# Third layer's experts: tiles ordered by the tokens they hold, and six of eight blocks of results added, turned and stored between the last tiles

## The chip, the core and the metric

The kernel runs on one core of one Trainium2 chip. The metric is the device time of one execution in microseconds (us), as the median of several runs. The kernel before took 3433.5 us (median of three runs, 3429.64 to 3435.67).

The engines: PE is TensorE (PEld is its weight load), DVE is VectorE, ACT is ScalarE, POOL is GpSimd, and SP is the engine that here only issues DMAs. "SPq" and "ACTq" are the instruction queues of SP and ACT, where they issue DMAs.

## The reference, cut to what matters

The whole network is an image of 256 channels and 64 x 64 places (4096 tokens) that passes through two convolution layers, an attention layer with experts, and a second attention layer with experts. Only the last stage is touched: for each token, two of eight experts are chosen, each expert is a two-layer product with a GELU between, and the two weighted results are added to the token. Then tokens become channels again.

```python
gate_logits = xf @ Wg + bg
top_w, top_i = jax.lax.top_k(gate_logits, TOP_K)          # TOP_K = 2 of E = 8 experts
top_w = jax.nn.softmax(top_w, axis=-1)
...
for e in range(E):
    h = jax.nn.gelu(xf @ W1[e] + b1[e], approximate=False)    # 256 -> 1024
    out = out + w_dense[:, e:e + 1] * (h @ W2[e] + b2[e])     # 1024 -> 256
```

## The kernel before

**Tokens and blocks.** The 4096 tokens live on the chip in `t` (128 partitions x 32 rows of 256). A block is 512 tokens (`NB`), so there are eight (`NBLK`), each of four rows of 128 (`TPB`). The output is written as channels, one block of 512 columns at a time.

**From tokens to experts' tiles.** `route` (L2028, L2039) finds both experts of each token and scatters its row into `xs` in DRAM, where each expert has a list. `S["cum"]` counts how many rows each expert has so far. A tile is 256 rows of one expert's list (`MT`). There are at most 39 tiles (`NTILE`); 36 are always run (`MOST`), and the last three stand under a condition (L2279) and are skipped where the counts need no more. In this profile they are skipped.

**Two lists of tiles.** The first 20 tiles (`FULL`) are full with tokens of blocks 0 to 6 alone, whatever the data, so their list ("A", `full_table`, L2125) is made while the attention of the last block still runs. The others are listed in "B" by `tile_table` (L2157) as one of the `steps` that `attn3` hands to the experts. Both lists go expert by expert. The lists hold, for each tile, the row in `xs` and the expert; for a tile that is not full, `in` and `off` send the rows beyond the end to a place that nobody reads.

**The loop over tiles** (`expert_tiles`, L2282). Iteration i loads rows four tiles ahead and weights two ahead (both on SP's queue), then does `first(i)`, 32 matmuls into `f_h_ps` with a GELU on ACT (L2320); four transposes of tile i+1's rows (L2254) whose copy is L2255 on DVE; and `second(i-1)`, 56 matmuls into `f_ya_ps` and `f_yb_ps`, the additions on DVE (L2375 to L2384), a scaling on ACT (L2391), and two scatters on POOL (L2392) into `ys` in DRAM, one row for each token and choice. `sides` (L2349) prepares combinations of weights on POOL. Two steps are taken in each iteration while any are left; PE's order is as written until the last step has been taken, and from then on a planner orders all engines by priority (place in the program) and by when it thinks inputs are there. Until then PE alone is fixed; the others are the planner's.

**The end.** After the last tile and the condition, `store` (L1365) takes the eight blocks in turn. For each it loads the block's two results out of `ys` (`outputs`, L2438, one half by SP, one by ACT, 512 KB each), adds token and results in PSUM by three transposes into each place (`to_channels`, L244, so 24 for a block), copies half 0 with ACT (L254) and half 1 with DVE (L256), and stores 512 KB (L1375). In `to_channels` a half of four places fills one bank of PSUM.

A read of `ys` waits for all scatters ahead of it in the program, since a scatter's rows are known only at run time. For the same reason a scatter behind a read waits until that read has landed.

Of the kernel before, what the change touches and what calls it, by code (L numbers as in the profile page):

```python
# [10 lines left out]
F32 = mybir.dt.float32  # L11
BF16 = mybir.dt.bfloat16
I32 = mybir.dt.int32
AF = mybir.ActivationFunctionType
ALU = mybir.AluOpType
# [4 lines left out]
P = 128  # L20
C = 256
# [71 lines left out]
class Net:  # L93
# [1270 lines left out]

    def store(self, t, out, more=False):  # L1365

        with (
            self.tc.tile_pool(name="st", bufs=3) as pool,
            self.tc.tile_pool(name="st_ps", bufs=2, space=PSUM) as ps,
        ):  # L1370
            for b in range(NBLK):
                o = pool.tile([P, 2, NB], F32, tag="o", name="st_o")
                y = self.outputs(b, pool.tile([P, 2, TPB, C], F32, tag="g", name="f_g")) if more else None
                self.to_channels(ps, "ps", t[:, b * TPB : (b + 1) * TPB, :], o, *([y[:, 0], y[:, 1]] if more else []))
                self.nc.sync.dma_start(out=out.rearrange("(m p) n -> p m n", p=P)[:, :, b * NB : (b + 1) * NB], in_=o)  # L1375

# [582 lines left out]
    def moe_consts(self, pool):  # L1963
# [6 lines left out]
                                channel_multiplier=-1, compare_op=ALU.is_ge, fill=0.0)  # L1970
        i = pool.tile([P, NTILE], I32, tag="count_i", name="count_i")
        nc.gpsimd.iota(i, pattern=[[1, NTILE]], base=0, channel_multiplier=0)
        self.count = pool.tile([P, NTILE], F32, tag="count", name="count")
        nc.vector.tensor_copy(self.count, i)
# [64 lines left out]
    def route_parts(self, t0, T, t, S, wp, n, nT, bank):  # L2039
# [47 lines left out]
        def count():  # L2087
            hot = got["hot"]
            both = got["both"] = room("f_both")[:, :T]
            nc.vector.tensor_add(both, hot[:, 0], hot[:, 1])  # L2090

            cum = got["cum"] = wp.tile([P, TPB + 1, NE], F32, tag="f_cum", name="f_cum")
            if t0 == 0:
                nc.vector.memset(cum[:, 0, :], 0.0)
            else:
                nc.vector.tensor_copy(cum[:, 0, :], S["cum"])
            for i in range(T):
                nc.vector.tensor_add(cum[:, i + 1, :], cum[:, i, :], both[:, i, :])
            S["cum"] = cum[:, T, :]

# [23 lines left out]

    def full_table(self, S, wp, bank):  # L2125

        nc = self.nc
        T, n = S["A"], FULL
        tl = lambda shape, tag, dt=F32: wp.tile([P] + shape, dt, tag="f_" + tag, name="f_" + tag, bufs=1)
        c_ps = bank()[:, :NE]  # L2130
        self.mm(c_ps, [(self.all_one, S["cum"])])
        ci = tl([NE], "ci", I32)
        nc.vector.tensor_copy(ci, c_ps)
        nc.vector.tensor_single_scalar(ci, ci, MT.bit_length() - 1, ALU.arith_shift_right)
        full = tl([NE], "cnt")
        nc.vector.tensor_copy(full, ci)
        ends = tl([NE], "ends")
        nc.vector.tensor_tensor_scan(ends, self.one.to_broadcast([P, NE]), full, 0.0, ALU.mult, ALU.add)
        past = tl([NTILE, NE], "past")[:, :n]
        nc.vector.tensor_tensor(past, bc(ends, 1, n), bc(self.count[:, :n], 2, NE), ALU.is_le)  # L2140
        nc.vector.tensor_reduce(T["ex"], past, AX.X, ALU.add)
        nc.vector.tensor_scalar_mul(T["tab"][:, 0, :], T["ex"], float(P))
        nc.vector.tensor_tensor(past, past, bc(full, 1, n), ALU.mult)
        tau = tl([NTILE], "tau")[:, :n]
        nc.vector.tensor_reduce(tau, past, AX.X, ALU.add)
        nc.vector.tensor_sub(tau, self.count[:, :n], tau)
        nc.vector.tensor_scalar_mul(tau, tau, float(MT))
        nc.vector.scalar_tensor_tensor(tau, T["ex"], float(N), tau, ALU.mult, ALU.add)
        nc.vector.tensor_copy(T["tab"][:, 1, :], tau)
        gone = S["gone"]  # L2150
        nc.vector.tensor_sub(gone, full, ends)
        nc.vector.tensor_scalar(gone, gone, float(n), 0.0, ALU.add, ALU.max)
        nc.vector.tensor_tensor(gone, gone, full, ALU.min)
        nc.gpsimd.memset(T["in"], 1.0)
        nc.gpsimd.memset(T["off"], 0.0)

    def tile_table(self, S, wp, bank, early=False):  # L2157


        nc = self.nc  # L2160
        T = S["B"]
        n = NTILE - FULL if early else NTILE
        tl = lambda shape, tag, dt=F32: wp.tile([P] + shape, dt, tag="f_" + tag, name="f_" + tag, bufs=1)
# [8 lines left out]
        nc.vector.tensor_copy(cnt, ci)  # L2172
        if early:
            nc.vector.tensor_sub(cnt, cnt, S["gone"])
        ends = tl([NE], "ends")
# [15 lines left out]
        nc.vector.tensor_sub(tau, tau, skip)  # L2191
        if early:
            nc.vector.tensor_tensor(past, bc(ex, 2, NE), bc(self.count[:, :NE], 1, n), ALU.is_equal)
            nc.vector.tensor_tensor(past, past, bc(S["gone"], 1, n), ALU.mult)
            nc.vector.tensor_reduce(skip, past, AX.X, ALU.add)
            nc.vector.tensor_add(tau, tau, skip)
        nc.vector.tensor_scalar_mul(tau, tau, float(MT))
# [14 lines left out]
        nc.vector.tensor_tensor(ins, bc(self.nth[:, :NI], 1, n), bc(skip, 2, NI), ALU.is_lt)  # L2212
        nc.vector.tensor_scalar(off, ins, -1.0, 1.0, ALU.mult, ALU.add)
        for i in range(0, n, 4):
            k = min(4, n - i)
            part = off[:, i : i + k, :].rearrange("p i k -> p (i k)")
            nc.vector.scalar_tensor_tensor(part, self.nth[:, : k * NI], float(2 * N), part, ALU.add, ALU.mult)

# [18 lines left out]
    def expert_where(self, T, j, x, tl):  # L2237
# [6 lines left out]
        op.tensor_tensor(to, x[:, :, C], second, ALU.add)  # L2244
        op.tensor_tensor(to, to, T["in"][:, j, :], ALU.mult)
        op.tensor_tensor(at, to, T["off"][:, j, :], ALU.add)
        op.tensor_tensor(first, first, x[:, :, C + 1], ALU.mult)
# [34 lines left out]
    def expert_tiles(self, S, order, wp, ps, steps, early, pre, written):  # L2282
# [119 lines left out]

        nc.scalar.activation(wp.tile([P, 1], F32, tag="g", name="f_gelu", bufs=1), self.one, AF.Gelu)
        xs, ws = {}, {}
        for i in tiles[:ahead_x]:
# [13 lines left out]
        for i in tiles:  # L2419
            if i + ahead_x <= tiles[-1]:  # L2420
                xs[i + ahead_x] = rows(i + ahead_x)
            if i + ahead <= tiles[-1]:
                ws[i + ahead] = weights(i + ahead)
            w1, w2 = ws.pop(i)
            xs.pop(i)
            h = first(xT, w1, (pre["ahead"][1:] if i == 0 else ()) if steps else None)
            now = (i, h, w2, sides(w2)) + to
            step()
            if i < tiles[-1]:
                xT = turn(xs[i + 1])  # L2430
                to = where(i + 1, xs[i + 1])
            if done is not None:
                second(*done)
                step()
            done = now
        second(*done)

    def outputs(self, b, y):  # L2438

        src = self.ys[: 2 * N, :].rearrange("(r b p i) c -> b p r (i c)", r=2, b=NBLK, i=TPB)  # L2440
        for r in range(2):
            (self.nc.sync, self.nc.scalar)[r].dma_start(out=(y[r] if isinstance(y, list) else y[:, r]).rearrange("p i c -> p (i c)"), in_=src[b][:, r])
        return y
# [9 lines left out]
    def moe_state(self, pool, L=2):  # L2453
        tl = lambda shape, tag, dt=F32: pool.tile([P] + shape, dt, tag=tag, name="f_" + tag)
        return {
            "L": L, "to": tl([2, NT], "to", I32), "used": tl([1], "used", I32),
            "big": tl([2, 2, NT // 2], "big"), "r": tl([NT], "r"), "gone": tl([NE], "gone"),
            **{k: {"tab": tl([2, n], "tab" + k, I32), "ex": tl([n], "ex" + k), "in": tl([n, NI], "in" + k), "off": tl([n, NI], "off" + k)}
               for k, n in (("A", FULL), ("B", NTILE))},
        }  # L2460
# [35 lines left out]

    def attn3(self, t, S):

# [5 lines left out]
        with (  # L2504
# [28 lines left out]
            if True:  # L2533
# [230 lines left out]
                with tc.manual_schedule(engines={ET.PE, ET.Pool}):  # L2764
                    steps = iter(())
                    for g in range(first, G + LAG):
# [6 lines left out]
                        if b > 0:  # L2773
# [6 lines left out]
                            if b == NBLK - 1 and j == TPB + 5:  # L2780
                                self.full_table(S, keep, bank)
                                one = lambda shape, tag: keep.tile([P] + shape, F32, tag=tag, name="f_" + tag, bufs=1)
# [8 lines left out]
            last = route((NBLK - 1) * TPB, TPB)  # L2791
            go = lambda: next(last, None)
            self.experts(
                S, [go] * 5 + [lambda: self.tile_table(S, keep, bank, True)],
                {**pre, "ahead": [lambda i=i: finish(NBLK - 1, i) for i in range(TPB)]},
            )

    def limits3(self, S, pool):
# [86 lines left out]
    def run(self, x, out):  # L2885
        tc, nc = self.tc, self.nc
        with tc.tile_pool(name="const", bufs=1) as cpool, ExitStack() as left:
# [20 lines left out]
            with tc.tile_pool(name="tok", bufs=1) as tpool:  # L2908
# [5 lines left out]
                with tc.tile_pool(name="moe", bufs=1, side="right") as mpool:  # L2914
# [4 lines left out]
                    with tc.tile_pool(name="weights2", bufs=1) as wpool:  # L2919
                        self.rows(wpool, "qk_scale", "wo_b")  # L2920
                        self.weights(wpool, ["w_qkv2", "w_o2"])
                        self.attn2(t, S)
                    self.attn3(t, S)
                    self.limits3(S, mpool)
                    flag = self.flag(cpool)

                    self.store(t, out, True)
            self.general(flag, xd, out)
# [122 lines left out]
```

## Time and profile before

| | us |
|---|---|
| median of three runs | 3433.5 |
| profiled execution, device time | 3392.35 |
| span of the profiled execution, first to last instruction | 3390.5 |
| mean granted clock of TensorE in it | 0.957 |
| PE busy in the span | 3089.0 (91%) |
| PEld busy | 2316.8 (68%) |
| DVE busy | 2300.9 (68%) |
| ACT busy | 1330.4 (39%) |
| POOL busy | 1460.4 (43%) |
| moved by DMA | 407.01 MB, mean 120 GB/s |

The profiled execution is 41.15 us (1.2%) shorter than the median of the runs. Times inside the profile are counted from the span's start. The third layer's experts run from about 2824 us to 3343 us, and the stores of the output from there to the end.

### The profile page before, as it was taken

How to read it: one execution, taken by the hardware profiler on the slowest of the kernel's cores; microseconds unless marked ns; L12 is line 12 of the kernel's file. 1: busy time of each engine (PE TensorE's matmuls, PEld its weight loads, DVE VectorE, ACT ScalarE, POOL GpSimd, SP SyncE). 2: the span in 40 equal slices, each digit the busy share in tenths (PEclk: the TensorE clock that was granted, in tenths of full speed). 3: DMA queues.
4: the chain of work that ended last, by engine and by line, in shares of the span. 5: the costliest groups of instructions: out<-in, count | busy, mean ns of one | idle time of the engine just before them, and what ended most of it. 6: DMA issues, size and time to landing. Idle time of an engine off the chain costs nothing.

```text
span 3390.5 us, 66220 instructions
## 1 busy us (share of the span) xinstructions
PE 3089.0 (91%) x25774; PEld 2316.8 (68%) x25774; DVE 2300.9 (68%) x5331; ACT 1330.4 (39%) x2552; POOL 1460.4 (43%) x1318
## 2 busy tenths in 40 slices
PE   6789999999977899797969799999999998999997
PEld 3443444344435888765858567888888887899996
DVE  8885677577764677787866576777777776555552
ACT  4444343434425666343644352222222223233331
POOL 2028787788852555434444352000000013555552
PEclk9889999999988999998979899999999999999998
DMA  2146655621134222200159653323333234555554
GB/s 72 43 110 146 160 153 157 152 61 52 50 108 122 66 75 74 60 1 2 51 170 288 210 188 126 98 91 97 100 100 100 81 94 162 190 197 210 209 197 177
DMA packets 241688, 407.01 MB, mean 120 GB/s; under 512 B 78353, under 2 KB 152850, under 8 KB 231890
## 3 DMA queue, kind: packets, MB, share of 16 engines
q1 hardware_dynamic: 212002, 344.40, 32.6%
q0 software_dynamic: 13056, 35.93, 2.8%
q10 hardware_dynamic: 16304, 22.31, 2.0%
q8 instruction: 207, 3.39, 0.4%
q14 instruction: 119, 0.97, 0.1%
HBM read 287.07 MB, written 111.30 MB: 117 GB/s over the span
## 4 chain that ended last, share of the span: by engine, by line
PE 47%; DVE 8%; DMA 4%; ACT 3%; issue 3%; POOL 2%; SPq 0%; POOLq 0%; DVEq 0%; ACTq 0%
PE f_h_ps L152 8%; PE a_sa_ps L2667 6%; PE f_ya_ps L152 3%; PE l_acc_ps L1160 3%; PE a_oa_ps L2706 3%; PE a_ob_ps L2706 3%; PE a_oc_ps L2706 3%; PE a_sb_ps L2667 3%; PE f_yb_ps L152 3%; DVE l_pr L1156 2%; PE a_q_ps L152 1%; PE a_od_ps L2706 1%; PE a_sc_ps L2667 1%; DMA ys<-f_y,f_at 1%; PE a_qkv_ps L152 1%
## 5 line engine op out<-in xcount | busy, mean ns | idle before, releaser
L776 ACT COPY l_sc<-l_s 128x384 f32<-128x384 f32 (+1 forms) x632 | 303.9, 532 | 454.1 <-PE l_s L769 444.5
L781 DVE TENSOR_TENSOR l_sm<-l_s,mask 128x256 f32<-128x256 f32 (+2 forms) x628 | 307.9, 550 | 90.8 <-PE l_s L769 89.7
L152 PE MATMUL f_h_ps<-f_xT,f_w 128*128 128x256 f32 x1440 | 339.2, 387 | 15.7 <-ACT f_h L2320 10.9
L2117 POOL DMA_INDIRECT xs<-f_room,f_to x64 | 64.3, 1004 | 642.3 <-DVE a_e L2654 476.0
L152 PEld LDWEIGHTS f_h_ps<-f_xT,f_w 128*128 128x128 f32 x1440 | 264.5, 192 | 71.4 <-ACT f_h L2320 27.9
L769 PE MATMUL l_s<-l_q,l_k 32*128 32x256 f32 (+3 forms) x2944 | 270.6, 452 | 0.0
L2686 ACT ACTIVATE a_e<-a_e 128x512 f32<-128x512 f32 x256 | 156.0, 630 | 253.7 <-DVE a_e L2656 249.9
L786 POOL TENSOR_TENSOR l_sm<-l_sc,mask 128x768 f32<-128x768 f32 (+1 forms) x116 | 202.5, 1754 | 87.8 <-ACT l_sc L776 87.6
L2320 ACT ACTIVATE f_h<-f_h_ps,f_w 128x256 f32<-128x256 f32 x360 | 166.3, 470 | 181.9 <-PE f_h_ps L152 173.6
L1156 DVE TENSOR_TENSOR l_pr<-l_vk,l_w_ps 128x1280 f32<-128x1280 f32 x128 | 186.5, 1481 | 54.3 <-PE l_acc_ps L1160 35.0
L769 PEld LDWEIGHTS l_s<-l_q,l_k 32*128 32x128 f32 x2944 | 132.5, 183 | 115.2 <-issue 67.2
L2392 POOL DMA_INDIRECT ys<-f_y,f_at x144 | 149.0, 1035 | 129.9 <-ACT f_y L2391 100.0
L1160 PE MATMUL l_acc_ps<-ident,l_pr 128*128 128x128 f32 x1600 | 198.3, 278 | 6.3 <-POOL l_pr L1151 6.2
L1160 PEld LDWEIGHTS l_acc_ps<-ident,l_pr 128*128 128x128 f32 x1600 | 184.9, 144 | 12.9 <-POOL l_pr L1151 7.9
L790 POOL TENSOR_TENSOR l_sm<-l_sc,mask 128x256 f32<-128x256 f32 (+1 forms) x220 | 185.0, 870 | 15.7 <-ACT l_sc L776 14.8
L2349 POOL TENSOR_TENSOR f_wt<-f_w 128x512 f32<-128x512 f32 x72 | 89.9, 1268 | 225.9 <-PE f_ya_ps L152 193.8
L2667 PE MATMUL a_sa_ps<-a_q,a_kt 128*128 128x256 f32 x512 | 156.9, 388 | 20.8 <-DVE a_u L2672 15.5
L2671 ACT COPY a_u<-a_sa_ps 128x256 f32<-128x256 f32 x128 | 47.6, 372 | 291.0 <-PE a_sa_ps L2667 291.0
L815 PE MATMUL l_b_ps<-l_sm,l_v 128*32 128x256 f32 (+2 forms) x2176 | 153.5, 372 | 0.0
L2667 PE MATMUL a_sa_ps<-a_qt,a_kt 128*128 128x256 f32 x512 | 153.4, 381 | 0.0
L786 POOL TENSOR_TENSOR l_sm<-l_sc,mask_c 128x768 f32<-128x768 f32 (+1 forms) x64 | 121.1, 1908 | 38.9 <-ACT l_sc L776 38.2
L2667 PE MATMUL a_sb_ps<-a_qt,a_kt 128*128 128x256 f32 x512 | 132.3, 381 | 0.0
(590 smaller groups left out, 7267.7 us busy)
## 6 DMA issues: line engine op xcount, KB each, us to landing
a_kt<-a_kd SPq DMA_DIRECT2D x128, 512.0 KB
f_w<-in_f_w SPq DMA_DIRECT2D x36, 1152.0 KB
f_w<-in_f_w SPq DMA_DIRECT2D x36, 1028.0 KB
xs<-zero SPq DMA_DIRECT2D x8, 4160.0 KB
l_vk<-vt SPq DMA_DIRECT2D x180, 128.0 KB
f_x<-xs SPq DMA_DIRECT2D x72, 260.0 KB
f_w<-in_f_w SPq DMA_DIRECT2D x36, 384.0 KB
l_rcp<-l_recd SPq DMA_DIRECT2D x48, 256.0 KB
```

The lines of the kernel that those rows point to most:

```text
L152: self.nc.tensor.matmul(out, lhsT, rhs, start=(i == 0), stop=(i == len(pairs) - 1))
L769: nc.tensor.matmul(s[pair, j][:, at : at + m, :], key(hp), qs[hp], start=(z == 0), stop=(z == len(pieces) - 1))
L776: nc.scalar.copy(sc[:, j], s[1, j])
L781: nc.vector.tensor_tensor(to(pair, j, kind, at), pick(s[pair, j], kind, which), mask, ALU.mult)
L786: nc.gpsimd.tensor_tensor(out[:, :, at, :], of[:, :, which, :], bc(mask, 1, 2), ALU.mult)
L790: nc.gpsimd.tensor_tensor(to(1, j, kind, at), pick(sc[:, j], kind, which), mask, ALU.mult)
L1156: nc.vector.tensor_tensor(pr, vk, bc(held["w"][:, j, dy], 3, D), ALU.mult)
L1160: nc.tensor.matmul(acc[:, m, j, :], pf[:, dx, m * P : (m + 1) * P], self.ident, is_transpose=True, start=(j == 0 and dy == 0 and dx == 0 a ...
L2320: nc.scalar.activation(h[:, m, :], p[:, m % 2, :], AF.Gelu, bias=w1[:, 2 * hidden + m : 2 * hidden + m + 1])
L2667: mm = lambda out, i, right: nc.tensor.matmul(out, A[i], right, start=True, stop=True)
L2686: nc.scalar.activation(e[:, i : i + 3 : 2], e[:, i : i + 3 : 2], AF.Exp, scale=1.0 / 16.0)
L2706: nc.tensor.matmul(out, vs[:, j, i, :], right, start=(j == 0 and side != 1), stop=(j == NPAIR - 1 and side != 0))
```

## The change

1. `route` keeps the counts after each block (`S["cums"]`) instead of only the newest.
2. Both lists are made by `list_tiles`, in two parts: up to a matrix `put`, then one matmul that brings it to all partitions, and the tables from it. The order of tiles is by block first and by expert inside: list A takes tiles in the order in which blocks complete them; list B takes what is left in the order of the first blocks whose tokens they hold. List A needs no `in` and `off`. The first part of A stays at the same place of the attention's loop, and the second follows one turn later, with the load of the first tile behind it. B's step becomes two steps.
3. So block b's results are complete after a number of tiles that is known before the run. At iterations 29 to 34 the loop calls `read(b)` for blocks 0 to 5, between the transposes of tile i+1 and `second(i-1)`: two loads of 512 KB out of `ys` on SP's queue into one buffer. One iteration later, behind `second`, it calls `give(b)`: two additions of 128 x 1024 on DVE into `t`, eight transposes into one PSUM bank (two halves), two copies, and a store of 512 KB on SP's queue.
4. `read(6)` stands ahead of the last `second`, `read(7)` behind the condition; both are divided between SP and ACT. Then both blocks are turned by 24 transposes each and stored, as before.
5. The counts for the flag (`limits3`, `flag`), which were ahead of the stores in the program, are now behind them.

```diff
-    def store(self, t, out, more=False):
...
-    def full_table(self, S, wp, bank):
...
+    def list_tiles(self, S, wp, bank, nm, n):
...
+        self.mm(c_ps, [(self.all_one, S["cums"][:, :G, :].rearrange("p b e -> p (b e)"))])
...
+            nc.vector.tensor_copy(upto[:, :NE], S["gone"])
+            nc.vector.tensor_tensor(by_block(have), by_block(ci), bc(S["gone"], 1, G), ALU.max)
+        new = tl(NBLK * NE, "new")[:, :K]
+        nc.vector.tensor_sub(new, have, had)
+        ends = tl(NBLK * NE, "ends")[:, :K]
+        nc.vector.tensor_tensor_scan(ends, self.one.to_broadcast([P, K]), new, 0.0, ALU.mult, ALU.add)
...
+        for r in range(lines):
+            nc.vector.tensor_scalar_mul(put[:, r, :], self.ident[:, :n], rows[:, r : r + 1])
+        yield
+
+        p = bank()[:, : lines * n].rearrange("p (r i) -> p r i", r=lines)
+        self.mm(p.rearrange("p r i -> p (r i)"), [(self.all_one, put.rearrange("p r i -> p (r i)"))])
+        nc.vector.tensor_scalar_mul(T["tab"][:, 0, :n], p[:, 0], float(P))
+        nc.vector.tensor_copy(T["tab"][:, 1, :n], p[:, 1])
+        nc.vector.tensor_copy(T["ex"][:, :n], p[:, 0])
...
@@ expert_tiles
+            for f in beside.get(i, ()):
+                f()
             if done is not None:
                 second(*done)
                 step()
+            for f in after.get(i, ()):
+                f()
             done = now
+        for f in beside.get(len(tiles), ()):
+            f()
         second(*done)
...
@@ attn3
                             if b == NBLK - 1 and j == TPB + 5:
-                                self.full_table(S, keep, bank)
+                                lists = self.list_tiles(S, keep, bank, "A", FULL)
+                                next(lists)
+                            if b == NBLK - 1 and j == TPB + 6:
+                                next(lists)
...
+            def send(b, o):
+                nc.sync.dma_start(out=channels[:, :, b * NB : (b + 1) * NB], in_=o)
+
+            def read(b, tag="room", size=TPB * CX + 2 * NB):
+                y = keep.tile([P, size], F32, tag=tag, name="f_" + tag, bufs=1)
+                ys[b] = self.outputs(b, y[:, : 2 * TPB * C].rearrange("p (r i c) -> p r i c", r=2, c=C), (nc.sync, nc.scalar if b > NBLK - 3 else nc.sync))
+
+            def give(b):
+                y = ys.pop(b)
+                part = t[:, b * TPB : (b + 1) * TPB, :]
+                for r in range(2):
+                    nc.vector.tensor_tensor(part, part, y[:, r], ALU.add)
+                o = keep.tile([P, 2, NB], F32, tag="oT", name="st_o", bufs=1)
+                self.to_channels(keep_ps, "q", part, o)
+                send(b, o)
+
+            beside, after, i = {}, {}, 0
+            for b in range(NBLK - 1):
+                i = max(i + 1, FULL + max(NE, 4 * (b + 1) + NE - 1 - FULL) + 1)
+                beside.setdefault(i, []).append(lambda b=b: read(b))
+                if i < MOST:
+                    after.setdefault(i + 1 if i + 1 < MOST else i, []).append(lambda b=b: give(b))
+            assert i == MOST
             self.experts(
-                S, [go] * 5 + [lambda: self.tile_table(S, keep, bank, True)],
-                {**pre, "ahead": [lambda i=i: finish(NBLK - 1, i) for i in range(TPB)]},
+                S, [go] * 5 + [more] * 2,
+                {**pre, "ahead": [lambda i=i: finish(NBLK - 1, i) for i in range(TPB)], "beside": (beside, after)},
             )
+            read(NBLK - 1, "w2", 9 * C)
+            with tc.tile_pool(name="st_ps", bufs=2, space=PSUM) as ps:
+                for b in (NBLK - 2, NBLK - 1):
+                    y = ys.pop(b)
...
+                    self.to_channels(ps, "ps", t[:, b * TPB : (b + 1) * TPB, :], o, y[:, 0], y[:, 1])
+                    send(b, o)
...
                     self.limits3(S, mpool)
                     flag = self.flag(cpool)
-
-                    self.store(t, out, True)
```

## Prediction

> **What bounds the kernel now.** First the busy shares in 40 slices (about 85 us each; a digit is tenths), to see which engine fills the experts' stage and what happens in the last slice:
> ```profile
> PE   6789999999977899797969799999999998999997
> DVE  8885677577764677787866576777777776555552
> DMA  2146655621134222200159653323333234555554
> ```
> PE is full until the last slice; DVE and DMA have room. Then the stretches around the end (columns: PE, PEld, DVE, ACT, POOL busy, clock, DMA share, GB/s):
> ```profile
> 3250.00:3300.00 50.00, 50.00 (x330) 45.56 (x330) 25.43 (x58) 19.02 (x44) 30.45 (x24) 1.00 0.51 187
> 3300.00:3350.00 50.00, 40.28 (x298) 37.51 (x296) 19.84 (x42) 12.26 (x29) 19.42 (x17) 0.92 0.26 92
> 3350.00:3391.00 41.00, 26.61 (x190) 24.96 (x190) 5.53 (x8) 4.69 (x8) 0.00 (x0) 0.83 0.74 283
> ```
> While tiles run, PE never rests, so whatever PE gets there costs its whole length. In the last 41 us it is mostly DMA. The chain that ended last says what those wait for (start, length, what):
> ```profile
> 3345.94 4.39 DMA f_g<-ys
> ...
> 3350.47 4.94 PE tr_ps L251 x22
> ...
> 3365.37 10.89 DMA f_g<-ys
> ...
> 3376.31 7.00 PE tr_ps L251 x47
> ...
> 3383.39 0.69 DVE st_o L256
> ```
> So the stores run from the landing of the last scatter (3345.7) to the end (3390.5), 44.8 us, limited by loads of results, PE and stores in turn. The last product ends at 3339.5; I call that E. From E to the end: 51.0 us.
>
> Next the timeline of one tile, to see which queue issues what, and when:
> ```profile
> 3196.46 1.06 PE L152 MATMUL f_yb_ps<-f_w,f_hs 128*128 128x128 f32 x8
> 3198.52 1.24 DVE L2384 TENSOR_TENSOR f_y<-f_y,f_w 128x512 f32<-128x512 f32 x1
> 3199.97 0.33 SPq L2234 DMA_DIRECT2D f_w<-in_f_w  x1
> 3202.39 1.25 POOL L2392 DMA_INDIRECT ys<-f_y,f_at  x1 [0.15 <-ACT f_h L2320]
> ```
> A tile takes 13.62 us. T is the end of its `second` on PE (3197.5): SP issues the second weights at T+2.5, after the addition that frees their buffer, and POOL scatters at T+4.9 and T+6.4.
>
> Last, a warning from tile 4, where DVE stood before a row load that had not landed:
> ```profile
> 2893.83 0.60 DVE L2240 TENSOR_SCALAR f_first<-f_x,f_exA 128x2 f32<-128x2 f32 x1 [8.40 <-DMA f_x<-xs]
> 2900.61 3.78 PE L152 MATMUL f_h_ps<-f_xT,f_w 128*128 128x256 f32 x8 [8.08 <-ACT f_h L2320]
> ```
> DVE held 8.4 us became PE held 8.1 us. This is what the change could repeat six times.
>
> **What the Trainium skill says.** "DMA: Bandwidth & Descriptors", Issuing engines are not separate DMA queues: loads issued from several engines share the same 16 DMA engines. The trace agrees: in the stores SP and ACT load halves together, at a share of 0.74 for 283 GB/s. "Perfetto Trace Analysis", Matmuls: matmul groups should rotate through PSUM banks, so that evacuation overlaps. `give` has one bank, the old store two; no row here shows one. "VectorE: DVE Perf Modes" prices an fp32 addition of N columns at (N+151)/0.96 ns, 1224 ns for 1024; the trace has 1220 at L2559, and that is used.
>
> **The change part by part**, against the profiled execution (3392.35 us, span 3390.5).
>
> *The tail.* Four steps.
> - `read(6)` waits for the scatters of tile 34. The last began at 3337.07 and lands as the final one did (3343.33 to 3345.74, 2.4 us): 3339.5, at E. With issue it starts at E+0.2 and takes what the first pair took, 4.39: E+4.6. Its half on ACT's queue keeps ACT until E+0.2; behind it stand the last tile's first copy (E-0.8) and scaling (E+1.8). The copy, if placed behind, is 1 us late and the wait below still covers it.
> - The last tile's scatters stood at 3342.05, E+2.55. Being behind a read of the same buffer, they now wait until E+4.6: a new wait, on POOL; nothing is queued there behind it. From first issue to landing they took 3345.74-3342.05 = 3.7: E+8.3.
> - `read(7)`: issue 0.2, 4.4 us: E+12.9. Block 6 is turned meanwhile.
> - Block 7's 24 transposes took 4.94 us when PE was cold and about 2.6 at full clock (0.11 each). I take 4.0: E+16.9. Copy and issue 0.8: E+17.7. From the end of the last copy (3384.1) to the span's end 6.4: E+24.1.
>
> 51.0-24.1 = **-26.9 us**. Bounds: -29 if the scatters need not wait for `read(6)` (2.1 less), -23 if loads take 1 us more each and PE stays cold. `limits3` and `flag`, moved behind, are a dozen DVE operations of 0.13 to 0.6 us and a small matmul; before they ran as early as 2833 and 3339 though written later, and else lie under the last store's 6 us: nothing, or +3 uncovered.
>
> *PE in the loop.* Six blocks of eight transposes at 0.11 us (four of tile i+1's rows take 0.44 in the chain, at the same full clock): 48 x 0.11 = **+5.3 us**, in full, since PE is never idle there.
>
> *DVE and ACT in the loop.* Per block two additions of 1.22, a copy of 0.69 on DVE, one of 0.59 on ACT. DVE is busy 7.0 us of a 13.62 us tile (25.43/50); 3.1 more leaves 3.5 free. ACT is at 38%. Covered by PE's own 13.62 us, if nothing waits; uncovered it would be 3.1 us a block.
>
> *DMA in the loop.* Per block 1.05 MB read and 0.52 MB stored. At the tail's 283 GB/s and share 0.74 that is 1.57/0.283 x 0.74 = 4.1 us of all engines, 0.30 of a tile; on 0.51 to 0.62 this makes 0.8 to 0.9. Full, but below 1; weights have about 10 us from issue (T+2.5) to their use by `sides` at the next T. No price; +5 if bursts collide.
>
> *The waits in the loop.* `read(b)` waits on SP for the scatters of two tiles ago (landed at T-4.8) and for the buffer, which `give(b-1)` frees. If it stands behind the second weights, it issues at T+3; 1.18 MB of weights and 1.05 MB of results at the 380 to 415 GB/s of the fullest slices in the DMA view of these tiles, plus the 2.4 us that a scatter takes to land as an estimate of the fixed part, land at about T+11. Behind it on SP: rows and first weights, due more than a tile later. POOL's scatters, at T+4.9 before, wait until then and are issued by T+13.5 (1.5 apart), and behind them `sides` of the next tile, wanted at T+13.6, with a whole tile of reserve, since it prepares one tile ahead: it fits. `give(b)` stands behind the following `second`, so its transposes are due at T+13.6; additions 2.4 from T+11 give T+13.4. It just fits. The store behind them (0.38 on SP) waits for the copies, some 3 us into the next tile; behind it stand weights that a buffer keeps back until T+2.5 of that tile anyway. Between the halves PE waits about 0.9 us for ACT's copy of the one bank (0.59 and the hand-overs), unless products are planned in between. No row shows this: from 0 to 6 us a block (the additions planned behind `second`'s own, which end at T+2.2: 2.2+2.4+0.9). I take 0.5, because products of the next tile are there to fill: **+3 us**, bounds 0 and 36.
>
> *The lists.* A: about 24 small DVE operations of 0.15 to 0.22 us instead of 17, then a matmul in PE's fixed order one turn (6.05 us) later. The load of the first rows waits for `xs` until 2796.8 anyway, 8 us after the old table: hidden; +1 for PE waiting on `put`. B: some 30 operations before `put`, and its matmul stands ahead of tile 4's products, on an engine held 8.4 us just there. If `put` comes after the hold, 24 products (5.3 us) that ran during it move behind; against that, fewer list operations delay the additions afterwards. I take +2. Together **+3 us**, bounds -2 and +8.
>
> *Sum*: -26.9+5.3+3+3 = **-15.6 us**: 3376.8 for the profiled execution. The runs shown are 41 us (1.2%) above it; scaling by 1.012, -15.8: 3433.5-15.8 = **3418 us** (-0.46%).
>
> **The rivals.**
> - *The forecast*: most of the stores vanish from the end, little comes back. For it: 13.6 us of slack by the written order, PE's fixed pace. 3408 to 3426.
> - *Slower*: DVE, in its fixed order, stands before a result load that is late, holds the copy of f_xT (L2255) or the additions, and PE stops at each block. It decides above (26.9-5.3-3)/6 = 3.1 us a block. At 6.5 us: -26.9+5.3+39+3 = +20.4, 3454 us. For it: tile 4's hold. Against: there the load waited for scatters just issued; here they are a tile old.
> - *No change*: bursts of weights and results collide, and about 2.3 us a block and 5 us more are lost: -26.9+5.3+14+8 = +0.4, 3434 us. That blocks stay unread until the end, because the planner puts loads late, ends here too.
> - *More*: no wait in the tail, none in the loop, lists free: -29+5.3 = -23.7, 3409.5; inside the forecast's case.
>
> **How the numbers follow.** Within 0.2% (6.9 us) of 3433.5 is about what a measurement can't tell from no change. Forecast with its better end 0.62, no change 0.14, slower 0.24. The range takes in the better bounds (-29+5.3-2 = -25.7, 3407.5, so 3407) and reaches to 3442, into the slower case: 3442 is a loss of 8.4 us, or 4.5 us a block. I leave out some 0.05 below and 0.14 above, about half of the slower case. Faster, same and slower are the three cases' chances.
>
> **What would show it.** Right: in the last iterations PE gaps under 1 us beside eight transposes each, additions done before PE asks, from the last product to the end about 24 us, and scatters of the last tile held some 2 us by `read(6)`. Wrong: DVE idle "<-DMA f_room<-ys" for several us with PE idle behind it, tiles of 17 us and more from 29 on, `f_w` landing late, or a gap of over 6 us ahead of tile 4's products.

## The result, and the profile after

| | before | after |
|---|---|---|
| median, 11 runs each | 3435.19 us | 3443.34 us |
| ratio of after to before | | 1.0026, 95% interval 1.0017 to 1.0035 |
| profiled execution | 3392.35 us | 3443.34 us |

The kernel is 0.26% slower, some 9 us. The forecast was 0.46% faster.

The two profiles can't be subtracted as wholes. The first stretch of each where they part lies in the second layer, which the change leaves alone. The stretch from 1600 to 1900 us in the first profile of before (length, PE, PEld, DVE, ACT, POOL busy, clock, DMA share, GB/s):
```profile
1600.00:1900.00 300.00, 267.92 (x2475) 222.87 (x2464) 201.49 (x778) 142.97 (x292) 136.37 (x145) 0.92 0.53 173
```
and in a second profile of the same kernel, of an execution of 3438.71 us:
```profile
1600.00:1900.00 300.00, 252.57 (x2254) 208.70 (x2242) 174.09 (x675) 125.45 (x250) 115.55 (x124) 0.83 0.41 134
```
Same program, but the clock is 0.92 against 0.83, and the first turn of a second-layer tile falls at 1752 against 1799 us. So I compare only the third layer, whose tiles take the same 13.62 us in mid-loop of both, in two pieces: L, from the first turn of its tiles (L2254 before, L2301 after) to E, the end of the last product; and R, from E to the end of the span.

| us | before | after | difference |
|---|---|---|---|
| L | 520.8 | 555.2 | +34.4 |
| R | 51.0 | 27.7 | -23.3 |
| sum | 571.8 | 582.9 | +11.1 |

The 40 slices of after, to be set beside those of before:
```profile
PE   6779999999977999897959789999999998999996
DVE  8886777577754677796646576777777776555553
DMA  1145656421143222100139663223333224555564
```
At this grain nothing shows but a little more DVE and DMA in the last slices. The stretches around the end do show it (same columns as above; E is at 3413.48):
```profile
3290.00:3340.00 50.00, 41.74 (x270) 37.44 (x269) 32.06 (x66) 13.23 (x32) 24.88 (x18) 0.96 0.60 213
3340.00:3390.00 50.00, 45.55 (x292) 40.92 (x291) 24.76 (x36) 13.47 (x31) 21.97 (x16) 0.93 0.62 214
3390.00:3413.50 23.50, 19.42 (x141) 17.97 (x139) 9.09 (x18) 5.65 (x13) 6.24 (x6) 0.93 0.19 68
```
PE was busy 50.00 of 50 us while tiles ran; now it is idle for 8.3, 4.5 and 4.1 us. The DMA share is 0.60, not full. The timeline of the first tile with a block says why (start, length, instruction, idle before and its releaser):
```profile
3286.40 1.25 POOL L2439 DMA_INDIRECT ys<-f_y,f_at  x1 [0.16 <-ACT f_h L2367]
...
3287.95 0.97 POOL L2439 DMA_INDIRECT ys<-f_y,f_at  x1 [0.30 <-issue]
...
3293.42 0.81 SPq L2496 DMA_DIRECT2D f_room<-ys  x2
...
3294.08 1.06 PE L152 MATMUL f_yb_ps<-f_w,f_hs 128*128 128x128 f32 x8
...
3296.79 3.47 POOL L2396 TENSOR_TENSOR f_wt<-f_w,f_wt 128x512 f32<-128x512 f32 x2
...
3297.19 1.94 DVE L2867 TENSOR_TENSOR t<-t,f_room 128x1024 f32<-128x1024 f32 x1 [4.51 <-DMA f_room<-ys]
...
3299.79 1.55 DVE L2867 TENSOR_TENSOR t<-t,f_room 128x1024 f32<-128x1024 f32 x1
...
3301.91 0.69 DVE L2431 TENSOR_TENSOR f_y<-f_y,f_w 128x512 f32<-128x512 f32 x1
3302.63 0.91 ACT L2438 ACTIVATE f_y<-f_y,f_wgt 128x256 f32<-128x256 f32 x2 [4.37 <-DVE f_y L2431]
...
3303.45 1.18 ACT L2367 ACTIVATE f_h<-f_h_ps,f_w 128x256 f32<-128x256 f32 x3
...
3304.31 0.91 PE L152 MATMUL f_h_ps<-f_xT,f_w 128*128 128x256 f32 x3 [3.97 <-ACT f_h L2367]
...
3314.49 0.60 PE L251 MATMUL tr_ps<-ident,t 128*128 128x128 f32 x4
```
Read it from the line at 3304.31 backwards. PE waits 3.97 us for a GELU (L2367). That GELU stands on ACT behind the scaling of the tile before (L2438), which waits for the bias addition (L2431). That stands on DVE behind both additions of `give(0)` (L2867), which the planner put among the additions of the `second` that ends on PE at 3295.1. This is a whole tile earlier than where they are written: `give(0)` is called behind the next `second`, and its transposes, whose order on PE is fixed, come at 3314.49. DVE is free for the first addition at 3292.7 and waits 4.51 us for the result load; the two take 1.94 and 1.55 us, not 1.22, while POOL makes its side weights (L2396). Over all blocks, the list of waits from 3290 us on has (us in all, times, the longest):
```profile
ACT f_y L2438 <- DVE f_y L2431: 25.3, 8, 5.0
...
PE f_h_ps L152 <- ACT f_h L2367: 16.8, 6, 4.1
...
DVE t L2867 <- DMA f_room<-ys: 13.1, 5, 4.5
```
So there are two suspects for one chain: additions that stand ahead of their load, and additions that are long. The rival to both is traffic, or PE's own added work.

At tile 4, where DVE stood 8.40 us before a row load, the timeline now has the list as well:
```profile
2934.73 0.87 DVE L2284 TENSOR_SCALAR f_first<-f_x,f_exA 128x2 f32<-128x2 f32 x1 [8.85 <-DMA f_x<-xs]
...
2939.34 0.68 PE L152 MATMUL a_q_ps<-f_put,all_one 128*128 128x57 f32 x2 [5.65 <-DVE f_put L2190]
```
PE waits for list B's `put` in place of a GELU, and the interval from turn to turn is 26.59 us, not 23.74 (24.70 in the second profile of before).

In the tail the chain that ended last is still made of scatter, load, transposes and copy, but one link of each is left:
```profile
3420.80 2.42 DMA ys<-f_y,f_at
...
3423.37 5.64 DMA f_w<-ys
...
3429.05 4.10 PE tr_ps L251 x23
...
3433.17 0.69 DVE f_w L256
```

### The profile page after: what moved, and what is told of

Same layout as the page of the kernel before. It is cut to its first block, busy times and chain, and to the rows that moved or that the text cites. A ratio compares the mean times of both kernels' runs of the same rounds, so it can differ in the third digit from the quotient of the medians.

```text
span 3441.2 us, 66030 instructions
## 1 busy us (share of the span) xinstructions
PE 3117.4 (91%) x25682; PEld 2333.0 (68%) x25682; DVE 2317.2 (67%) x5338; ACT 1330.2 (39%) x2552; POOL 1466.2 (43%) x1316
## 5 line engine op out<-in xcount | busy, mean ns | idle before, releaser
L152 PE MATMUL f_h_ps<-f_xT,f_w 128*128 128x256 f32 x1440 | 348.9, 393 | 23.6 <-ACT f_h L2367 17.8
L2367 ACT ACTIVATE f_h<-f_h_ps,f_w 128x256 f32<-128x256 f32 x360 | 165.3, 470 | 192.0 <-PE f_h_ps L152 165.5
L2396 POOL TENSOR_TENSOR f_wt<-f_w 128x512 f32<-128x512 f32 x72 | 90.9, 1282 | 237.7 <-PE f_ya_ps L152 205.7
L2721 PE MATMUL a_sa_ps<-a_q,a_kt 128*128 128x256 f32 x512 | 156.5, 387 | 19.6 <-DVE a_u L2726 17.6
L2760 PE MATMUL a_ob_ps<-a_et,a_vs 128*128 128x256 f32 x512 | 132.5, 381 | 0.0
```

Source lines behind the costliest of these rows:

```text
L152: self.nc.tensor.matmul(out, lhsT, rhs, start=(i == 0), stop=(i == len(pairs) - 1))
L2367: nc.scalar.activation(h[:, m, :], p[:, m % 2, :], AF.Gelu, bias=w1[:, 2 * hidden + m : 2 * hidden + m + 1])
L2721: mm = lambda out, i, right: nc.tensor.matmul(out, A[i], right, start=True, stop=True)
```

## The experiments

Ratios are against the kernel before on the same chip, with 95% intervals; L and R come from the profile of each. They ran on four chips, four kernels on each; before itself takes 3437 us on A and B and 3393 us on C and D. "Late" means moved behind another operation; the sections below say which. The L of two profiles of one kernel differs by up to 2.8 us here (after), and R by up to 2.3, so a difference of that size between two of these kernels shows nothing by itself.

| kernel | chip | ratio | L | R |
|---|---|---|---|---|
| before, again | A | 0.9994 (0.9984 to 1.0005) | 520.7 | 49.6 |
| after, again | D | 1.0026 (1.0017 to 1.0034) | 552.4 | 30.0 |
| lists and order alone | A | 0.9999 (0.9989 to 1.0008) | 523.8 | 49.9 |
| no additions | A | 0.9954 (0.9937 to 0.9971) | 530.2 | 28.8 |
| additions late | A | 1.0002 (0.9992 to 1.0012) | 546.3 | 27.2 |
| additions late, no side weights | B | 0.9951 (0.9933 to 0.9970) | 530.4 | 28.9 |
| after, no side weights | C | 0.9998 (0.9989 to 1.0007) | 544.4 | 27.2 |
| sums on PE | B | 0.9991 (0.9981 to 1.0000) | 540.7 | 27.5 |
| additions and turning late | B | 0.9984 (0.9975 to 0.9993) | 540.4 | 24.7 |
| after, load 6 behind the scatters | B | 1.0024 (1.0017 to 1.0031) | 555.0 | 26.7 |
| additions late, third side buffer | C | 0.9957 (0.9940 to 0.9974) | 532.6 | 24.8 |
| the same, again | D | 0.9960 (0.9947 to 0.9974) | 530.6 | 24.8 |
| ... and turning late | C | 0.9957 (0.9943 to 0.9972) | 536.4 | 22.0 |
| ... and result load behind the scatters | C | 0.9988 (0.9979 to 0.9997) | 544.3 | 22.5 |
| before, third side buffer | D | 1.0015 (1.0009 to 1.0022) | 527.6 | 49.5 |
| after, third side buffer | D | 1.0008 (0.9998 to 1.0018) | 546.8 | 27.4 |

**The reference points.** Before, unchanged:

> The kernel before, unchanged, profiled once more. Theory S (its first profile was a short execution: the 41 us between its 3392 us and the timed runs lie ahead of the third layer's experts): this profile has a span near 3431 us, the first f_x transposes of the second layer's experts near 1789 us as in the changed kernel (1752 in the first profile), and from the last product to the end about 51 us. Rival: the first profile was typical and the changed kernel lost 37 us in the second layer: then 1752 again, and a span near 3391.

Span 3436.8 us, first turn of the second layer's tiles at 1799 us, R 49.6: the first profile was short ahead of the third layer, and the third layer is the same. After, unchanged, on chip D:

> The changed kernel, unchanged, on the chip of the next three: 1.0026 times the kernel before, as measured before.

The ratio repeats to the last digit, on a chip where both kernels are some 43 us faster. L is 552.4 this time, 2.8 us less than in the first profile, and R 30.0, 2.3 us more.

**Lists and order alone.** After's lists, with the output stored at the end as before:

> The changed kernel's lists and order of tiles, with the end of the kernel before: all eight blocks are added, turned and stored after the last tile. Theory C: lists and order cost about 6 us (3.6 in the first tiles, 2.5 in the attention ahead of them): 3441. If they are free, 3435; if the second layer was planned anew and slower for them, 3470.

L is 3.0 us longer, nearly all of it in the first six tiles; the ratio can't be told from 1, so the 6 us expected are not there. The second layer is not touched.

**Which engine holds the tiles.** First, `give`'s additions behind the bias addition (L2431, kept as `self.biased`) of the turn in which `give` is written, a tile later than the planner had them:
```diff
-                for r in range(2):
-                    nc.vector.tensor_tensor(part, part, y[:, r], ALU.add)
+                with tc.issue_after(self.biased.ins):
+                    for r in range(2):
+                        nc.vector.tensor_tensor(part, part, y[:, r], ALU.add)
```


> The changed kernel with one edit: the two additions by which give sums a block's results stand on DVE behind the bias addition of the same turn's second, not ahead of it. Theory A (DVE, in order, stands before a result load and holds the bias addition, behind it ACT's scaling, behind that the GELU that PE waits for; about 25 us over six blocks): tiles with a block fall from 16 to 21 us to some 15, the time from 3443 to about 3420. Rival B (the loss is the traffic of result reads and stores, and PE's own added work): the tiles stay at 17 to 21 us, 3441.

Neither: L falls by 8.9 of 34.4 us, and tiles with a block stay at 17.4 us or more. The load is not late for this place. For block 0 it is issued 17 us before the additions, which don't wait:
```profile
3304.09 0.81 SPq L2496 DMA_DIRECT2D f_room<-ys  x2
...
3321.03 4.49 DVE L2868 TENSOR_TENSOR t<-t,f_room 128x1024 f32<-128x1024 f32 x2
```
Now the changed kernel without its two additions, so that six blocks of the output lack their results:

> The changed kernel without the two additions per block (the results of blocks 0 to 5 are read but not added, so these blocks of the output lack them); reads, transposes, copies and stores are kept. Theory A: the hold is gone, some 3420. Rival B: 3441. If it falls further than the version with the additions moved, the rest is DVE's own time for them (2.4 to 4 us a block).

Tiles take 14.72 us each and the time is 0.46% below before. So traffic, transposes, copies and stores, all kept, are not the cause; they cost 14.72-13.62 = 1.10 us a block. The additions are, even where they no longer stand ahead of the bias addition. The timeline of the version with late additions, at the next block, shows what is left:
```profile
3338.80 1.24 DVE L2431 TENSOR_TENSOR f_y<-f_y,f_w 128x512 f32<-128x512 f32 x1
...
3339.46 3.92 POOL L2396 TENSOR_TENSOR f_wt<-f_w,f_wt 128x512 f32<-128x512 f32 x2
...
3339.96 4.49 DVE L2868 TENSOR_TENSOR t<-t,f_room 128x1024 f32<-128x1024 f32 x2
...
3344.60 0.63 PE L251 MATMUL tr_ps<-ident,t 128*128 128x128 f32 x4 [2.46 <-DVE t L2868]
```
DVE no longer waits for a load, but two additions take 4.49 us, not 2.44, and POOL's two beside them 3.92 in place of 2.5. PE, in its fixed order, stands 2.46 us before the transposes.

**Is it POOL?** The late version, with tiles from 30 on reusing tile 29's side weights:
```diff
-            now = (i, h, w2, sides(w2)) + to
+            wt = wt if L == 3 and i > 29 else sides(w2)
+            now = (i, h, w2, wt) + to
```


> The version with the additions behind the bias addition, but without POOL's side weights from tile 30 on (those tiles use tile 29's, so their outputs are other numbers); all else kept. Theory C (DVE's additions, 128x1024, take 2.25 us each beside POOL's L2396 and 1.22 alone[...]): each pair of additions ends 2 us earlier, tiles with a block fall from 17.4 to about 15.4, the time from 3438 to 3428. Rival: the 2.25 us come from the DMA traffic of that stretch: 3438.

More than expected. The same place then reads:
```profile
3329.18 0.69 DVE L2431 TENSOR_TENSOR f_y<-f_y,f_w 128x512 f32<-128x512 f32 x1
...
3329.80 2.48 DVE L2869 TENSOR_TENSOR t<-t,f_room 128x1024 f32<-128x1024 f32 x2
```
Both are at the length they have alone, with all loads and stores kept. L is 530.4, which is 520.8 and 3.0 for the lists and 6 x 1.10 for the transposes: no wait is left. The same left out of the changed kernel itself:

> The changed kernel without POOL's side weights from tile 30 on (those tiles use tile 29's, so their outputs are other numbers); the additions stay where the change has them. What is then left over the 14.7 us of a tile with its transposes is the wait for the result load alone. Theory D (both causes: the load's wait, 13 us by the record, and POOL's contention): 3443 falls to some 3432. If the wait on the load were the whole cause, 3443 stays; if contention were the whole cause, 3423, as with the additions moved.

L is 544.4: 14.0 us above 530.4, with additions of 1.22 us that wait 13.6 us for loads by the record. So the early place alone, with its wait for the load, costs 14.0 us; POOL alone, with the additions late, 546.3-530.4 = 15.9 us; and both together 555.2-530.4 = 24.8 us (22.0 in the second profile of after). They overlap; that an addition which waits for its load waits POOL out meanwhile would explain it, but isn't shown.

**Other ways round it.** Sums in PSUM, by 24 transposes a block and no addition on DVE:

> The changed kernel with the sums made on PE: 24 transposes a block that add up in PSUM, in place of two additions on DVE and eight transposes. Theory A: DVE no longer holds the bias addition; each block costs PE 24 x 0.11 = 2.6 us, tiles of 16.4 us where PE need not wait for the load itself: 3443 - 13 = 3430. If PE then stands before the result load in place of DVE (the load lands 4 us late at times), 3443 as before. Rival B (traffic): 3450.

Tiles of 16.78 us; PE does not stand before loads, and the better of the two outcomes is met within 0.2%. Late additions with the transposes one tile later:

> The version with the additions behind the bias addition, and in addition each block's turning (eight transposes on PE, two copies, the store) one tile later, behind the next second's products. Theory A2 (what is left there, 3 to 4 us a block, is PE in its fixed order standing before transposes whose additions are not done): tiles with a block fall from 17.4 to about 14.8 us, 13.62 and the transposes, as in the version without additions; from the first tile to the last product 546 becomes about 532, the time 3424. Rival B2 (the reads and stores of results, or ACT's copy between GELUs, hold PE): 17 us stay, 3438.

Half right. Two tiles take 13.62 and 14.72 us, two 20.56 and 19.23. In the two slow ones a DVE instruction is held for over 4 us just as POOL begins (the second of them here):
```profile
3364.08 4.31 DVE L2431 TENSOR_TENSOR f_y<-f_y,f_w 128x512 f32<-128x512 f32 x1
3364.11 2.49 POOL L2396 TENSOR_TENSOR f_wt<-f_w 128x512 f32<-128x512 f32 x2
```
Result loads ahead of the scatters hold POOL's queue up to 9.4 us here, and so move its side weights about.

**Move POOL's work instead.** A third buffer for the side weights, so that they need not wait for the end of the `second` that reads the old ones; the room comes from `f_hs`:
```diff
-tag="wt", name="f_wt", bufs=2)
+tag="wt", name="f_wt", bufs=3)
-tag="hs", name="f_hs", bufs=2)
+tag="hs", name="f_hs", bufs=1)
```


> The version with the additions behind the bias addition, and a third buffer for the side weights (f_wt), paid for by one buffer of f_hs in place of two. POOL's side weights then need not wait for the end of the second that reads the buffer, so they can be made before DVE's additions begin. Theory C (contention of POOL and DVE): tiles fall from 17.4 towards 14.8 us, 3438 to 3424 to 3430. Rival: POOL is held by scatters that wait for result loads, and starts its side weights as late as now: 3438.

0.43% below before, L 532.6. DVE's additions and POOL's side weights no longer meet:
```profile
3285.07 0.68 DVE L2431 TENSOR_TENSOR f_y<-f_y,f_w 128x512 f32<-128x512 f32 x1
...
3285.68 1.22 DVE L2868 TENSOR_TENSOR t<-t,f_room 128x1024 f32<-128x1024 f32 x1
...
3287.41 1.22 DVE L2868 TENSOR_TENSOR t<-t,f_room 128x1024 f32<-128x1024 f32 x1
...
3291.25 2.49 POOL L2396 TENSOR_TENSOR f_wt<-f_w 128x512 f32<-128x512 f32 x2 [7.16 <-DMA f_w<-in_f_w]
```
Repeated, and its parts alone:

> The version with both edits once more, in more runs: 0.9957 of the kernel before, some 15 us below it.

> The kernel before with a third buffer for the side weights and one for f_hs. Its tiles take 13.62 us with PE never idle, so contention is covered there: theory, no gain, 0.999 to 1.001, or 0 to 5 us lost where side weights now run beside other work of DVE. If 0.996, the gain of the better version has nothing to do with the change.

> The changed kernel with the third side buffer alone, its additions planned where they were. Theory D (both causes, the load's wait and POOL's contention, cost some 10 us each): as without side weights, 0.9998 of the kernel before, since DVE still stands before result loads. If contention were all, 0.9957.

The gain repeats (0.9960). On before, the buffer costs 0.15%: tiles in mid-loop take up to 0.8 us more, and one 3.9. On after alone it gives 1.0008; additions of 1.22 us, but DVE stands 8.38 and 8.20 us before two loads. So neither edit does it; both together do.

Two more on top of it:

> As the version before, with the turning of each block one tile later too. Theory C: 3422 to 3426, below the 3432 of two buffers. Rival as before: 3432.

> As the version before (third side buffer, additions and turning late), with each block's result load behind the scatters of the same turn, not ahead of them. The scatters need not wait for the load, so POOL starts the side weights early. If POOL's wait for the loads is what remains: 3420 to 3424. Against it: the load waits on SP for scatters just issued and lands some 5 us later, and weights stand behind it; if that is late for DVE or PE, 3440.

Late turning adds nothing. The load behind the scatters is worse: tiles of 15.4 to 17.6 us.

**The tail.** Load 6 moved behind the last `second` in the changed kernel:

> The changed kernel with block 6's result load behind the last tile's scatters, not ahead of them. Then the scatters need not wait for that load (they go at E+2.6 in place of E+6.0), but the load no longer runs beside the last tile. Expected from the last product to the end: scatters land at E+6.2, block 6 at E+11.4, block 7 at E+14, turned by E+19, end at E+26: 1 to 2 us below the 27.7 of the changed kernel, 3442. If the two loads get in each other's way fully, E+28: 3444.

R is 26.7: the wait of the scatters (3.5 us) and the overlap of the load nearly cancel. The ratio shows no difference from the changed kernel.

## Why the prediction was wrong

Its direction was wrong; its list of terms was nearly right. In us, against the profile:

| term | predicted | measured | from |
|---|---|---|---|
| tail | -26.9 | -23.3 | R, before and after |
| transposes in the loop | +5.3 | +6.6 | 6 x (14.72-13.62), no additions |
| lists | +3 | +3.0 | lists and order alone |
| waits in the loop | +3 (0 to 36) | +24.8 | L 555.2 less 530.4 |
| sum | -15.6 | +11.1 | |

The timed runs give +8.9 (0.26% of 3435), and the second profile of after 582.4-571.8 = +10.6. The tail alone gains 19.6 to 23.3 us, depending on which of the two profiles of each kernel are compared.

*The waits in the loop* is the step that failed, and 21.8 of the 26.7 us are in it. It was priced at 0.5 us a block and is 4.1, above the 3.1 from which the slower rival was said to decide. The slower rival had half of the mechanism: DVE in its order before a load that hasn't landed, an addition of `second` (the bias) held behind it, and PE behind that. It didn't name POOL. What the step assumed and what the runs showed:

- *The place of the additions.* The step set them between the landing of the load and the transposes ("additions 2.4 from T+11 give T+13.4. It just fits"), or at the worst behind the additions of the `second` of their own turn. The planner, which orders DVE here, put them a tile earlier. With T = 3295.1, the end of `second(28)`, ahead of which `read(0)` is written, DVE stood before the first at T-2.5, ahead of the bias addition of `second(28)`; the transposes came at T+19.4. The same early place is in all six blocks: all their additions run before the `second` ends behind which they are written. It costs 14.0 us without POOL.
- *The load* was not what failed. The step had it issued at T+3 and landed at T+11; it was issued at T-1.7 and DVE began to add it at T+2.1. The read did wait for scatters:
```profile
SPq L2496 <- DMA ys<-f_y,f_at: 7.1, 2, 6.6
```
  (SP's own waits from 3280 to 3300 us: in all, times, the longest.) From the start of the last scatter to the issue of the read are 5.5 us for block 0 and up to 7.8 for the others, where the step allowed 2.4 from the quiet end of the profile. In the written place this does no harm: without POOL's work the late version has no wait left.
- *The additions at 2.4 us a pair.* The price came from a row (L2559) beside which POOL rests, or begins only after the addition has begun. Their new place is beside POOL's side weights, and the profile of before had the warning, in the groups of DVE in mid-loop (busy time and mean ns, idle before):
```profile
L2384 DVE TENSOR_TENSOR f_y<-f_y,f_w 128x512 f32<-128x512 f32 x18 | 22.3, 1240 | 0.6
...
L2356 DVE TENSOR_TENSOR f_hs<-f_h 128x512 f32<-128x512 f32 x19 | 13.1, 691 | 41.9 <-ACT f_h L2320 41.9
```
  One operation and shape, 1240 ns where POOL's side weights run and 691 where they don't. L2384 itself takes 0.69 us in the last tile of before (at 3340.50), where POOL makes none. The Trainium skill, "SBUF — State Buffer", Who interferes with whom, says that a VectorE instruction with two SBUF inputs contends with a GpSimd instruction that reads SBUF, and that the order of issue decides which is blocked, while one with at most one SBUF input outside the two-port modes does not contend. The traces agree on who contends: additions of two SBUF inputs go from 1.22 to about 2.25 us, and L2425 (a PSUM and an SBUF input) takes 0.41 to 0.42 beside POOL or not. In two tiles they don't bear out the order (see the end).
- *The dear end of the bound*, "the additions planned behind `second`'s own", is the version with late additions, and it is 8.9 us better than what the planner did. The bound of 36 us holds the measured 24.8, by luck: it was worked out for another place.

*The tail* was right in its links, 3.6 us too short: `read(6)` holds the scatters until E+6.0, not E+4.6 (1.4), `read(7)` takes 5.64 and not 4.39 us (1.25), and from the end of the last copy to the end of the span it is 7.3 and not 6.4 (0.9). These are of one execution; in the other profile of after R is 30.0. The bound for no wait, 2.1 us less, is not reached: without that wait R falls by 1.0, less than the 2.3 by which R differs between the two profiles of after.

*Lists and transposes* held; a block's transposes cost 0.2 us more than their own length.

*The profile's own time.* Scaling by 1.012 hid a stretch of the second layer with another clock. It moved the result by 0.2 us and did no harm.

The forecast's amount did exist: with both waits taken away, the change gives 0.9957 and 0.9960 of before, 14 to 15 us.

## What to carry to other kernels

Slack on an engine is worth something only if the inserted work is ready when its turn comes. Where a planner sets the engine's order, that turn need not be the place in the program: price the early place as well as the late one, and pin an operation that waits for a DMA behind the operations on which other engines depend. Take the price of an operation from a row that has the same neighbours, not only the same shape; two rows of one shape with different means are a warning. An engine whose work is moved by a new wait can collide with another, so after moving work check what else runs in the new place. Here each repair alone left the time where before had it or above (1.0002 and 1.0008); only both together paid.

## What was not expected

- Sharing between DVE and POOL is not always in turns: beside late additions both slow down (4.49 and 3.92 us for two), but in two tiles of the version with late turning one DVE instruction was held for 4.24 and 4.31 us while POOL ran three of its own. Both had begun ahead of POOL's side weights in the trace (3364.08 against 3364.11 for the one shown), so the order of the starts there doesn't tell who is held. What decides it stays open.
- The same program takes 3437 us on two chips and 3393 on two others. In the two profiles of before nearly all of the difference lies in one stretch of the second layer; the ratio of after to before holds (1.0026 in both measurements).
